# One exponential over two neighbouring weight tiles in the encoder of a graph-attention kernel

## The chip, the cores and the metric

The kernel runs on one core of a Trainium2 chip. The metric is the device time of one execution in microseconds. Everything is float32 but the adjacency mask, which is held in bytes.

## The reference, cut to what matters

Two graph layers run over 4096 nodes with 512 features. The first is an attention autoencoder with four heads, the second a graph-attention layer. The first holds the change:

```python
h = jnp.maximum(_layernorm(x, axis=-1), 0.0)
Xw = jnp.einsum('hnd,hde->hne', Xh, W)                  # 4 heads of 128
f1 = jnp.einsum('hnd,hd->hn', Xw, V[:, 0, :, 0])
f2 = jnp.einsum('hnd,hd->hn', Xw, V[:, 1, :, 0])
sig = jax.nn.sigmoid(f1[:, :, None] + f2[:, None, :])
att = masked_softmax(adj * sig, adj != 0)               # 4096 x 4096 for each head
Xa = jnp.einsum('hij,hjd->hid', att, Xw)                # encoder
emb = mlp_block(batchnorm(Xa), enc_mlp_W, ...)          # elu, residual, batchnorm
Y = jnp.einsum('hij,hjd->hid', att, emb)                # decoder, the same att again
out = mlp_block(elu(Y @ W^T), dec_mlp_W, ...)
```

The exponent of the softmax is a sigmoid, so the kernel makes a weight as exp(0.5 * tanh(0.5 * (f1 + f2))) times the mask; a constant factor falls out in the softmax.

## The kernel before, in words

After a first stage (layer norm, the products with `w0`, the copy of the adjacency into byte masks in DRAM) comes the encoder's attention, then an MLP, the decoder's attention, a second MLP with the next layer's products, and that layer's attention. All three attentions go through the function `attention` (L222).

**A block.** `attention` runs over eight blocks: four heads times two halves of the targets, `TB` = 2048 each. In a block it runs over `NJ` = 32 groups of 128 sources. For each group j it makes a weight tile `e` of 128 sources by 2048 targets and multiplies the 128 values of these sources with it: four matmuls of 512 targets (L377), which add up in four PSUM banks over the 32 groups. The fourth bank comes into use two groups late (L371 to L375).

**A weight tile.** `tanh_weights` (L469) makes it in place with two ScalarE instructions and one of VectorE: a tanh (L471) of the row of target scores `rowb`, with the source's score as a bias for each partition, an exp (L472), and the product with the mask `a` (L473). The mask of a tile, 256 KB, is loaded on SP's queue (L211) into one of five buffers.

**The ring.** `weight_tile` (L253) hands out the tile's place: out of every `EP + ebufs` = 2 + 6 tiles, two come from the pool `keep`, which outlives the encoder, and six from the encoder's own pool. So a ring of eight places of 8 KB a partition goes round, and a tanh has to wait until everything that read the tile eight groups earlier is done.

**Who reads a tile.** The matmuls do, and so does the sum over sources that becomes the softmax's denominator. That sum is made in three ways, by lists of j (`ENC_FIRST`, `ENC_SECOND`, `ENC`): some tiles are added into a second sum by an accumulating DMA on POOL's queue in two halves (L392), some are multiplied with ones on PE (L266), and VectorE adds the others to `acc` (L400, L402). In blocks 2 to 7 eleven tiles go by DMA (j = 0, 2, 5, 7, 10, 12, 15, 17, 20, 22, 25), four by ones (8, 9, 30, 31) and seventeen by VectorE. At the end of a block PE folds both sums into the bank `den`. Every fifth tile is also stored to DRAM (L362), for the decoder: by ACT's queue in blocks 0 and 1, by SP's later.

**The end of a block** is worked off during the next one, at given j: VectorE copies the banks out (L583) and `den` (L272); POOL's queue carries `den` to DRAM (L273), back as columns (L278), VectorE inverts them (L282, L283), POOL's queue stores the inverses (L286) and spreads them over the partitions (L291), and VectorE scales the output (L587) and takes its statistics (L590). POOL's queue goes in order: while it waits for one of these, the accumulating DMAs behind it wait too.

**The order** of each engine's instructions comes from a scheduler that goes by the program's order and its own costs. `pinned` (L214) and `tc.issue_after` put the work of block ends behind given weights.

**The decoder** uses the same function with a ring of 2 + 4 places and reads every fifth tile back instead of making it. Its first two weight tiles lie in `keep`'s places, so that they can be made before the encoder's pool is let go.

Of the kernel before, what the change touches and what calls it, by code (L numbers as in the profile page):

```python
# [31 lines left out]
FP = mybir.dt.float32  # L32
U8 = mybir.dt.uint8
AF = mybir.ActivationFunctionType
ALU = mybir.AluOpType
# [4 lines left out]
N, F, H, D, P = 4096, 512, 4, 128, 128  # L40
IB = 512
NIB = N // IB
NJ = N // P
C = IB // P

TB = 2048
NTB = N // TB
SB = TB // IB
# [8 lines left out]
TINY = 1e-30  # L57
# [15 lines left out]
EP = 2  # L73
# [12 lines left out]
def kernel(ctx, tc, x, xT, adjT, w0, w0T, v0, wencT, wdecT, vecs, w1, w1T, a1, outT):  # L86
    nc = tc.nc
# [46 lines left out]
    score = consts.tile([P, 2, NTB, H, NJ // NTB], FP, name="score")  # L134
# [4 lines left out]
    def column(t, j, h):  # L139
        j = j % (NJ // NTB), j // (NJ // NTB)  # L140
        return t[:, j[1], h, j[0]:j[0] + 1]
# [10 lines left out]
    bias = consts.tile([P, C], FP, name="bias")  # L152
# [68 lines left out]

    def attention(what, keep, pools, weights, values, row_of, out, finish, ebufs, modes=None, invert=None,  # L222
                  kept=None, sums=None, sums2=None, extras={}, row0=None, masks0=(), in_parts0=1,
                  finish_last=None, behind=()):

# [18 lines left out]


        spool, made, masks0 = pools, 0, list(masks0)
        if invert is not None:
            acc = spool.tile([P, TB], FP, name="acc") if sums is None else sums  # L250
            sums2 = (spool.tile([P, TB], FP, name="acc2"), None) if sums2 is None else sums2

        def weight_tile():  # L253
            nonlocal made
            made += 1
            if (made - 1) % (EP + ebufs) < EP:
                return keep.tile([P, TB], FP, name="e", tag="ek", bufs=EP)
            return spool.tile([P, TB], FP, name="e", bufs=ebufs)


        hop = nc.scalar if kept is None else nc.gpsimd
# [60 lines left out]
        later, last_ones, last_main, products_of = {}, None, None, ()  # L322
        rowb = row0 if row0 is not None else next_row_of(0, 0)
        blocks = [(h, tb) for h in range(H) for tb in range(NTB)]
        for n, (h, tb) in enumerate(blocks):
# [8 lines left out]
            for j in range(NJ):  # L334
# [4 lines left out]
                with pinned([a_load, *products_of, last_main] if j else []):  # L339
                    if (n, j) in extras:  # L340
                        extras[n, j](a_load)
                    if not last and j == NJ - 10:
                        next_row = next_row_of(*blocks[n + 1])
                e = weight_tile()
                store = j % KEEP == KEEP - 1 and kept is not None
                if store and kept == "read":
                    a_load = nc.sync.dma_start(e, ekeep[h][tb][j // KEEP])
                else:
                    if masks0:
                        a, a_load = masks0.pop(0)  # L350
                    else:
                        a = mask_tile(keep)
                        a_load = load_mask(a, tb, j)

                    with pinned([*(products_of[:1] if kept == "read" and n == 0 and j < 8 else ()),
                                 *(behind if n == 0 and j < EP else ())]):
                        products_of = weights(e, rowb, a, j, h, SB if NJ * n + j < in_parts0 else 1)


                    if stores and (store if n > 1 else j % KEEP == KEEP - 3):  # L360
                        k, t = stores.pop()
                        (nc.sync if n > 1 else nc.scalar).dma_start(ekeep[h][tb][k], t)  # L362
                    if store:
                        stores.append((j // KEEP, e))
# [60 lines left out]
            if not last:  # L425
# [5 lines left out]
                rowb = next_row  # L431
# [37 lines left out]
    def tanh_weights(e, rowb, a, j, h, parts):  # L469
# [3 lines left out]
            last_dve = nc.vector.tensor_mul(e, e, a)  # L473
        return last_act, last_dve

    a_att, b_att, a_mlp, b_mlp = (coefs[:, k, :] for k in range(4))

    with tc.tile_pool(name="keep", bufs=1) as keep:

        with tc.tile_pool(name="f_small", bufs=1) as small, tc.tile_pool(name="f_work", bufs=2) as work:  # L480
            xs = []
# [4 lines left out]
            for ib in range(NIB):  # L486
# [7 lines left out]
                for c in range(0, C, 1 if ib == 0 else C):  # L494
                    n = 1 if ib == 0 else C
# [11 lines left out]
            for ib in range(NIB):  # L507
# [15 lines left out]
                for c in range(C):  # L523
                    if ib == 0 and c == 1:
# [3 lines left out]
                    made = (nc.gpsimd if by_pool else nc.vector).tensor_scalar(  # L528
                        hn, xs[ib][:, c, :], mv[:, c, 0:1], rstd[:, c:c + 1], ALU.subtract, ALU.mult)
# [23 lines left out]
                for c in range(C):  # L553
                    j = ib * C + c
# [12 lines left out]
                if ib == SB - 1:  # L567
                    store_rows(rows[0], targets(0))
                    row0 = keep.tile([P, TB], FP, name="rowb", bufs=2)
                    row0_load = load_row(row0, rows[0], 0)  # L570
                    with tc.issue_after(row0_load.ins):
                        masks0 = []
                        for j in range(5):
                            a = mask_tile(keep)
# [46 lines left out]
        with tc.tile_pool(name="enc", bufs=1) as spool:  # L621

            with tc.issue_after(last_copy.ins), tc.issue_after(masks0[-1][1].ins):
                attention("enc", keep, spool, tanh_weights, R[0:4], lambda h, tb: (rows[tb], h), out_enc,
                          (scaled, statistics), 6, lambda n: (ENC_FIRST, ENC_SECOND, ENC)[min(n, 2)],
                          (TINY, ALU.max), "write", row0=row0, masks0=masks0,
                          extras={(2, 8): encoder_weights, (H * NTB - 1, 10): coefs_of_three,
                                  (H * NTB - 1, 12): bias_of_three, (H * NTB - 1, 20): scale_three})

# [43 lines left out]
        with tc.tile_pool(name="m_small", bufs=1) as small, tc.tile_pool(name="m_work", bufs=3) as work:  # L673
# [8 lines left out]
            behind_it = []  # L682
# [46 lines left out]
        nc.sync.dma_start(w, wdecT.rearrange("(c p) o -> p c o", p=P))  # L729
        with tc.tile_pool(name="dec", bufs=1) as spool:  # L730
            attention("dec", keep, spool, tanh_weights, xc, lambda h, tb: (rows[tb], h), out_dec, (scaled, elu), 4,
                      kept="read", behind=behind_it, extras={(1, 6): sums_of_weights, (1, 16): bias_of_decoder})


    v1 = xd
# [2 lines left out]
    with tc.tile_pool(name="l_small", bufs=1) as small, tc.tile_pool(name="l_work", bufs=2) as work:  # L738
# [41 lines left out]
        for fb in range(C):  # L780
            with tc.issue_after(last_pe.ins):
                for h in range(H):
                    k = 2 * (fb * H + h)
# [232 lines left out]
```

## Time and profile before

| | |
|---|---|
| time, median of 3 runs (3245.06 to 3245.82) | 3245.78 us |
| span of the profiled execution, first to last instruction | 3243.0 us |
| what the median has beyond that span | 2.8 us |
| PE busy in the span | 3189.8 us (98%) |
| VectorE (DVE) busy | 2665.7 us (82%) |
| ScalarE (ACT) busy | 2582.4 us (80%) |
| encoder's attention | about 58 to 1038 us |
| tanh, L471, 128x2048 | 462 times, 1990 ns each |
| exp, L472, 128x2048 | 462 times, 1901 ns each |
| product with the mask, L473 | 470 times, 2260 ns each |
| TensorE clock granted | 0.997 |

The profile gives no time of its own for the profiled execution other than its span. Its rows tell the engine, the line, the operation, the tiles it writes and reads, their sizes and how often it ran; then the busy time or the mean of one, and the idle time of the engine just before, with what ended it. In a timeline the first number is the start in us from the start of the span, the second the duration. PE's records are halves of a float32 matmul, so four matmuls are eight records. The ends of matmuls are modelled: neighbouring records overlap.

### The profile page before, as it was taken

The numbers are of one execution on the slowest core, as the hardware profiler recorded it, in microseconds if no ns is written. First come the engines' busy times: TensorE is split into PE (matmuls) and PEld (weight loads), VectorE is DVE, ScalarE is ACT, GpSimd is POOL, SyncE is SP. The second block draws the span as 40 slices with busy tenths as digits, with TensorE's granted clock in tenths as the row PEclk, the third lists the DMA queues.
The fourth block names the chain that finished last, engine by engine and source line by source line (L and its number), as shares of the span: only waits on it lengthen the run. The fifth ranks groups of instructions, "written<-read, shape, count | busy, mean of one in ns | idle before, by whom it ended". The sixth has DMA issues, their size and how long they took to land.

```text
span 3243.0 us, 26057 instructions
## 1 busy us (share of the span) xinstructions
PE 3189.8 (98%) x8707; PEld 1480.1 (46%) x8707; DVE 2665.7 (82%) x1946; ACT 2582.4 (80%) x1825; POOL 478.3 (15%) x624
## 2 busy tenths in 40 slices
PE   7999999999999999999999999999999999999998
PEld 6334444444444464444444444448644444444443
DVE  7989999999998765555655665585699999999998
ACT  7999999999997559899999999566765656665663
POOL 3001211211210000000000000025412222122221
PEclk9999999999999999999999999999999999999999
DMA  9998988988985024444443443231489999899996
GB/s 211 198 198 243 276 225 230 270 225 227 265 240 150 7 72 143 136 130 136 142 151 126 128 154 126 73 124 59 127 206 221 208 231 236 217 216 234 232 211 160
DMA packets 212023, 580.60 MB, mean 179 GB/s; under 512 B 25168, under 2 KB 28272, under 8 KB 195888
## 3 DMA queue, kind: packets, MB, share of 16 engines
q0 software_dynamic: 68256, 223.56, 36.4%
q1 hardware_dynamic: 132200, 332.53, 30.2%
q10 hardware_dynamic: 11432, 22.85, 2.0%
q8 instruction: 68, 1.11, 0.1%
q14 instruction: 67, 0.55, 0.0%
HBM read 378.15 MB, written 84.30 MB: 143 GB/s over the span
## 4 chain that ended last, share of the span: by engine, by line
PE 50%; DVE 26%; issue 13%; DMA 6%; ACT 4%; DVEq 0%; POOL 0%; ACTq 0%; POOLq 0%; SPq 0%
PE ps L377 36%; DVE e L933 8%; DVE R L402 8%; PE ps L639 7%; DVE e L473 4%; DVE acc L402 3%; PE ps L838 3%; DMA a<-mask 3%; DMA acc<-e 2%; ACT e L471 2%; ACT e L472 1%; DMA w<-e 1%; PE den L266 1%; PE ps L699 1%; PE ps L374 1%
## 5 line engine op out<-in xcount | busy, mean ns | idle before, releaser
L377 PE MATMUL ps<-e,R 128*128 128x512 f32 x6008 | 2608.3, 595 | 25.8 <-DVE e L473 21.5
L377 PEld LDWEIGHTS ps<-e,R 128*128 128x128 f32 x6008 | 1137.4, 190 | 1490.2 <-issue 1395.7
L473 DVE TENSOR_TENSOR e<-e,a 128x2048 f32<-128x2048 f32 (+1 forms) x470 | 1053.0, 2260 | 392.4 <-ACT e L472 369.4
L471 ACT ACTIVATE e<-rowb,score 128x2048 f32<-128x2048 f32 (+1 forms) x470 | 911.8, 1968 | 82.9 <-PE ps L377 45.4
L472 ACT ACTIVATE e<-e 128x2048 f32<-128x2048 f32 (+1 forms) x470 | 869.3, 1879 | 8.0 <-DVE e L473 2.7
L932 ACT ACTIVATE e<-rowb,nq,jcol 128x2048 f32<-128x2048 f32 x224 | 459.6, 2088 | 262.4 <-DMA w<-e 143.5
L933 DVE SCALAR_TENSOR_TENSOR e<-e,jcol,a 128x2048 f32<-128x2048 f32 (+1 forms) x265 | 592.6, 2269 | 2.8 <-ACT e L932 2.8
L402 DVE TENSOR_TENSOR R<-R,e 128x2048 f32<-128x2048 f32 x128 | 292.3, 2283 | 0.0
L402 DVE TENSOR_TENSOR acc<-acc,e 128x2048 f32<-128x2048 f32 x121 | 276.3, 2283 | 0.9
L392 POOL DMA_DIRECT2D w<-e x178 | 149.4, 845 | 611.4 <-DMA w<-e 285.0
L639 PE MATMUL ps<-R,w 128*128 128x512 f32 x512 | 220.3, 592 | 0.6 <-DVE w L597 0.6
L392 POOL DMA_DIRECT2D acc<-e x146 | 122.7, 891 | 521.8 <-DMA acc<-e 217.3
L291 POOL DMA_DIRECT2D rb<-rinvs x60 | 34.0, 571 | 1055.9 <-DVE R L587 871.5
L639 PEld LDWEIGHTS ps<-R,w 128*128 128x128 f32 x512 | 97.2, 190 | 122.7 <-issue 117.4
L660 ACT ACTIVATE ex<-ps,bias 128x512 f32<-128x512 f32 x64 | 44.0, 688 | 100.7 <-PE ps L639 80.9
L838 PE MATMUL ps<-w1x,hT 128*128 128x260 f32 x512 | 115.5, 384 | 1.4 <-ACT hT L816 1.4
L838 PEld LDWEIGHTS ps<-w1x,hT 128*128 128x128 f32 x512 | 96.5, 190 | 19.9 <-issue 3.3
L932 ACT ACTIVATE e<-w,nq,jcol 128x2048 f32<-128x2048 f32 (+1 forms) x41 | 67.4, 1711 | 24.6 <-DMA R<-e 24.5
L875 POOL TENSOR_TENSOR vacc<-vacc,R 128x128 f32<-128x128 f32 x120 | 65.9, 579 | 45.2 <-ACT R L868 44.9
L662 DVE SCALAR_TENSOR_TENSOR ex<-ex,re 128x512 f32<-128x512 f32 x64 | 44.9, 702 | 32.8 <-ACT re L661 32.7
L868 ACT ACTIVATE R<-ps,rstd 128x128 f32<-128x128 f32 x128 | 38.6, 371 | 29.2 <-PE ps L838 25.5
L266 PE MATMUL den<-e,ones 128*32 128x512 f32 x416 | 51.7, 608 | 3.2 <-DVE e L933 3.2
(176 smaller groups left out, 1239.6 us busy)
## 6 DMA issues: line engine op xcount, KB each, us to landing
a<-mask SPq DMA_DIRECT2D x720, 256.0 KB, 4.1
w<-e POOLq DMA_DIRECT2D x178, 512.0 KB, 6.7
acc<-e POOLq DMA_DIRECT2D x146, 512.0 KB, 7.0
e<-ekeep SPq DMA_DIRECT2D x48, 1024.0 KB, 4.9
ekeep<-e SPq DMA_DIRECT2D x36, 1024.0 KB, 7.0
mask<-in_adjT POOLq DMA_DIRECT2D x8, 2048.0 KB, 104.7
rowb<-rows SPq DMA_DIRECT2D x16, 1024.0 KB, 5.4
rb<-rinvs POOLq DMA_DIRECT2D x60, 256.0 KB, 4.7
```

The lines of the kernel that those rows point to most:

```text
L266: last_ones = nc.tensor.matmul(den[s * 32:(s + 1) * 32, :], ones[:, 0:32], t[:, s * IB:(s + 1) * IB], start=start, stop=stop)
L377: last_main = nc.tensor.matmul(b, block(values[h], j), e[:, s * IB:(s + 1) * IB], start=(j == 0), stop=(j == NJ - 1))
L392: nc.gpsimd.dma_start(into_half, e_half, **({"accum_op": ALU.add} if j > moved[0] else {}))
L402: nc.vector.tensor_add(acc, acc, e)
L471: nc.scalar.activation(e, rowb, AF.Tanh, bias=column(score[:, 1], j, h), scale=0.5)
L472: last_act = nc.scalar.activation(e, e, AF.Exp, scale=0.5)
L473: last_dve = nc.vector.tensor_mul(e, e, a)
L639: last = nc.tensor.matmul(z, w[:, fb, o * P:(o + 1) * P], nodes(src[fb], ib), start=(fb == 0), stop=(fb == C - 1))
L838: m = nc.tensor.matmul(banks[k][:, 0:2 * DX], hT[:, fb, c * P:(c + 1) * P], w1x[:, fb, 2 * k:2 * k + 2, :].rearrange("p h x -> p (h x)"), ...
L875: nc.gpsimd.tensor_add(vacc[:, h, :], vacc[:, h, :], block(v1[h], j))
L932: last_act = nc.scalar.activation(e, rowb, AF.Relu, bias=column(nq, j, h), scale=column(jcol, j, h))
L933: last_dve = nc.vector.scalar_tensor_tensor(e, e, column(jcol2, j, h), a, ALU.add, ALU.mult)
```

## The change

Both parts of the ring become one tensor each: `ring`, two places, in `keep`, for the encoder and the decoder; and `ring2`, six places, in the encoder's pool. A place is a slice of its tensor.

In the encoder, all tiles but the first two are made in pairs (j even and j + 1). At the even j, `slots_of_two` takes two neighbouring places, and `tanh_pairs` writes two tanhs into them, each with its own bias, and then one exp over both, 4096 elements a partition. The product with the mask stays one instruction for each tile, at its own j. The places of a pair are separate slices, so each is waited for and let go by itself. The decoder keeps `tanh_weights`; it takes its two kept places from `ring`, too. The third attention is as before.

```diff
+        ring2 = spool.tile([P, ebufs, TB], FP, name="er") if pairs is not None else None
...
         def weight_tile():
             nonlocal made
             made += 1
-            if (made - 1) % (EP + ebufs) < EP:
-                return keep.tile([P, TB], FP, name="e", tag="ek", bufs=EP)
-            return spool.tile([P, TB], FP, name="e", bufs=ebufs)
+            k = (made - 1) % (EP + ebufs)
+            if k < EP:
+                return ring[:, k, :] if ring is not None else keep.tile([P, TB], FP, name="e", tag="ek", bufs=EP)
+            return ring2[:, k - EP, :] if pairs is not None else spool.tile([P, TB], FP, name="e", bufs=ebufs)
+
+        def slots_of_two():
+
+            nonlocal made
+            k = made % (EP + ebufs)
+            made += 2
+            return ring[:, k:k + 2, :] if k < EP else ring2[:, k - EP:k - EP + 2, :]
...
-                e = weight_tile()
+                by_two = pairs is not None and n * NJ + j >= EP
+                if not by_two:
+                    e = weight_tile()
+                elif j % 2:
+                    e = two[:, 1, :]
+                else:
+                    two = slots_of_two()
+                    e = two[:, 0, :]
...
-                        products_of = weights(e, rowb, a, j, h, SB if NJ * n + j < in_parts0 else 1)
+                        if not by_two:
+                            products_of = weights(e, rowb, a, j, h, SB if NJ * n + j < in_parts0 else 1)
+                        else:
+                            if j % 2 == 0:
+                                last_act = pairs(two, rowb, j, h)
+                            products_of = last_act, nc.vector.tensor_mul(e, e, a)
...
+    def tanh_pairs(two, rowb, j, h):
+
+        for k in range(2):
+            nc.scalar.activation(two[:, k, :], rowb, AF.Tanh, bias=column(score[:, 1], j + k, h), scale=0.5)
+        both = two.rearrange("p k i -> p (k i)")
+        return nc.scalar.activation(both, both, AF.Exp, scale=0.5)
...
     with tc.tile_pool(name="keep", bufs=1) as keep:
+        ring = keep.tile([P, EP, TB], FP, name="ek")
...
-                          (TINY, ALU.max), "write", row0=row0, masks0=masks0,
+                          (TINY, ALU.max), "write", row0=row0, masks0=masks0, ring=ring, pairs=tanh_pairs,
...
-                      kept="read", behind=behind_it, extras={(1, 6): sums_of_weights, (1, 16): bias_of_decoder})
+                      kept="read", behind=behind_it, ring=ring, extras={(1, 6): sums_of_weights, (1, 16): bias_of_decoder})
```

More of the change, by code (lines that the diff above doesn't have):

```diff
@@ L223, in attention @@
                   kept=None, sums=None, sums2=None, extras={}, row0=None, masks0=(), in_parts0=1,
-                  finish_last=None, behind=()):
+                  finish_last=None, behind=(), ring=None, pairs=None):
         spool, made, masks0 = pools, 0, list(masks0)
+        ring2 = spool.tile([P, ebufs, TB], FP, name="er") if pairs is not None else None
         if invert is not None:
```

## The prediction

> **What bounds the kernel now.** I read the engine table, then the busy time by stage, because the change touches only the encoder's attention (58 to about 1038 us of the span). Blocks are the eight (head, half) passes of that loop, n = 0 to 7. The view of stages gives one block a row (columns: PE, PEld, DVE, ACT, POOL, then clock and DMA). First the page's engine line, then two of these stages:
>
> ```profile
> PE 3189.8 (98%) x8707; PEld 1480.1 (46%) x8707; DVE 2665.7 (82%) x1946; ACT 2582.4 (80%) x1825; POOL 478.3 (15%) x624
> ```
>
> ```profile
> 555.00:673.00 118.00, 116.56 (x304) 49.50 (x304) 114.16 (x63) 118.00 (x65) 22.39 (x29) 1.00 0.89 241
> 673.00:791.00 118.00, 116.56 (x304) 49.50 (x304) 114.15 (x64) 118.00 (x65) 22.36 (x29) 1.00 0.89 241
> ```
>
> The page as a whole says PE. These stages say ACT: 118.00 of 118.00 us, with PE 1.4 us and DVE 3.9 us short of full. The view of waits for ACT alone has no entry at all from 405 to 1026 us. Before that, from 192 us, it has:
>
> ```profile
> ACT e L471 <- PE den L266: 4.5, 4, 2.0
> ACT e L471 <- DMA acc<-e: 2.7, 2, 2.5
> ACT e L472 <- DVE e L473: 2.7, 3, 1.3
> ```
>
> So until 400.35 us (the last of these waits) ACT is held by the ring: it waits for a place that PE's ones-products or an accumulating DMA has not yet let go. From then on it runs without a pause. Its rhythm, in the timeline of ACT (start, duration), first in the encoder, then in the decoder:
>
> ```profile
> 597.90 3.88 ACT L471 ACTIVATE e<-rowb,score 128x2048 f32<-128x2048 f32 x2
> 601.69 3.70 ACT L472 ACTIVATE e<-e 128x2048 f32<-128x2048 f32 x2
> 605.29 3.88 ACT L471 ACTIVATE e<-rowb,score 128x2048 f32<-128x2048 f32 x2
> ```
>
> ```profile
> 1499.21 1.99 ACT L471 ACTIVATE e<-rowb,score 128x2048 f32<-128x2048 f32 x1
> 1501.23 1.91 ACT L472 ACTIVATE e<-e 128x2048 f32<-128x2048 f32 x1
> 1503.04 1.99 ACT L471 ACTIVATE e<-rowb,score 128x2048 f32<-128x2048 f32 x1
> ```
>
> Two tanhs, two exps, 605.29 - 597.90 = 7.39 us for a pair of tiles, 16 pairs 118.2 us: the block. In the decoder an exp stands right behind the tanh that it reads, and starts 2.02 us after it instead of 1.89: such a direct dependence costs 0.13 us.
>
> PE at its fastest: 64 records of L377 take 27.47 us in the chain that ended last, 0.429 each; a block has 256, so 109.9, and 48 ones records at 3.57/32, so 5.4: 115.2 us. PE is next, 3.0 us below ACT.
>
> **What the Trainium skill says.** "ScalarE: Activation LUTs", What ACT_TABLE_LOAD costs: an ACTIVATE with immediate operands takes 186 ns + 0.833 ns per element, a pointer bias adds about 93, and neighbours overlap by about 93. The trace agrees: 1.99 us for tanh (pointer bias), 1.90 for exp, and starts 1.89 and 1.80 apart. Its Table sets section puts tanh and exp in one set; no load stands between them here. "Perfetto Trace Analysis", Identifying the Most-Contended Engine, warns that matmul busy time is no measure of PE's headroom: hence the 115.2 from spacing above. "DMA: Bandwidth & Descriptors", Rules for kernel authors: an accumulating DMA must wait for the earlier one's semaphore. The trace has 217 us of POOL waiting for `acc<-e` landings in the encoder: a serial chain.
>
> **The change part by part.**
>
> *Fewer exps.* 127 pairs lose two exps of 2048 and gain one of 4096. No 4096 form is in the trace; by the page it is 186 + 3412 - 93 = 3505 ns from start to start (an estimate), against 2 x 1800. Gain 0.093 us a pair (bounds: 0, if the second half brings its own start-up; 0.186, if nothing overlapped). I take 0.093.
>
> *Order on ACT.* In the built program 114 of the 127 double exps stand behind one tanh of the next pair, 13 right behind their own second tanh. Those 13 pay 0.13 each (bounds 0 and 0.25), and the tanhs queued behind them with them; DVE alone waits for the exp itself. A steady block has 16 pairs and two such: 16 x 0.093 - 2 x 0.13 = 1.23, so 118.2 becomes 117.0, still above PE's 115.2 and DVE's 114.2.
>
> *What of it counts.* Up to 400.35 us ACT is held by the ring, and a gain there only lengthens the wait. From there (tile 89 of 256) I count to where the end is decided. From 909.54 us, the last tile of block 6, PE runs without a gap to the end of the encoder:
>
> ```profile
> 905.14 3.70 PE L377 MATMUL ps<-e,R 128*128 128x512 f32 x8 [0.70 <-DVE e L473]
> 907.21 6.68 DVE L473 TENSOR_TENSOR e<-e,a 128x2048 f32<-128x2048 f32 x3
> ...
> 909.54 2.84 PE L377 MATMUL ps<-e,R 128*128 128x512 f32 x6 [0.70 <-DVE e L473]
> ```
>
> That start is set by DVE, which last waited for ACT (0.69 us, in DVE's timeline) at 847 us, tile 16 of block 6. Pairs from tile 89 to there: 60 x 0.093 = 5.6, less 8 direct ones x 0.13 = 1.0: 4.5 us, unrounded. What ACT gains later PE doesn't pass on.
>
> *Later first product.* A pair's multiplications now wait for both tanhs, one more tanh, and the double exp: 3 x 1.89 + 3.60 = 9.3 us after the first tanh, against 5.7 (two tanhs, one exp). DVE runs 3.6 us further behind ACT, for both tiles, since the second product follows the first. At the start of the encoder this is covered: DVE there waits 12.0 us in all for masks. Wherever DVE follows ACT again (after 346 us) it is paid once, not per block, and is still there at 907 us: +3.6. Bounds 1.8 (if the extra tanh weren't ahead) and 4.0. Cover gone at the start, nothing more: the same shift isn't paid twice.
>
> *Places freed one by one.* The waits in the built program stand at each tanh for its own place (accumulate semaphores only where that place's last user was accumulated), so the wider tiles add none. But a double exp is queued behind the first tanh of the next pair, and its wait for a place. Nobody waits there after 405 us now. The nearest place is one read by an accumulating DMA, on POOL's queue, block 5:
>
> ```profile
> 705.41 0.58 POOL L286 DMA_DIRECT2D rinvs<-dcol  x1 [1.80 <-DVE dcol L283]
> 710.49 1.63 POOL L291 DMA_DIRECT2D rb<-rinvs  x3 [4.49 <-DMA rinvs<-dcol]
> 712.10 1.85 POOL L392 DMA_DIRECT2D acc<-e  x2
> 721.35 0.84 POOL L392 DMA_DIRECT2D acc<-e  x1 [7.40 <-DVE acc L402]
> ```
>
> POOL waits for DVE's reciprocal, and everything behind it, down to tile 15's accumulate (second half issued at 734.20, landed 743.6), moves by DVE's 3.6. Tile 23's tanh, which takes that place, starts at 747.53: slack 3.9 us. It also comes 0.9 us sooner in its block (24 tanhs x 0.04), so 4.5 of slack is asked for. By the same reckoning blocks 4 and 6 have 5.7 and 4.9, block 7 over 8. One block misses by 0.6; with landings that scatter (2.9 to 11.4 us there) I take 1.0 us (bounds 0 and 12). In block 2, where the chain binds already, rinvs isn't waiting for DVE, so nothing moves.
>
> *PE, SP and the decoder.* PE's order is unchanged; DVE's too in blocks 3 to 6; SP moves one row load by one place; POOL moves one accumulate a block past a neighbour. The decoder keeps its single exps; only the name of its two kept tiles changes. All costed at nothing.
>
> **Sum.** Against the profiled execution: -4.5 + 3.6 + 1.0 = +0.1 us on a span of 3243.0. The median of the runs, 3245.78, is 2.8 above that span (what lies outside first and last instruction), which I carry over: 3245.9.
>
> **Rivals.** *No change that can be told (forecast, 0.74).* As above. What a measurement of this kernel can tell is about 0.2%, 6.5 us.
>
> *Faster (0.06).* The latency isn't paid, because PE's last stretch starts elsewhere, and the ring's waits before 400 us shrink too: all 127 pairs, 11.8 - 13 x 0.13 = 10.1 us, 3235.7. For it: ACT is full. Against: PE has 3 us a block left and is without a gap in block 7.
>
> *Slower (0.20).* The accumulate chain takes ACT's place as the bound. Place: the tanhs of tiles 20, 23 and 25 of blocks 3 to 6, behind POOL's wait for DVE. It decides from where the slack falls below 4.5 us. If landings there are 2 to 3 us later than now, each of four blocks loses some 3 us: 3245.9 - 1.0 + 12 = 3256.9. For it: slack 3.9 in block 5, and DMA engines 89% busy. Against: the shift is paid as a delay once a block, and most landings have more room.
>
> *That it doesn't do what it says:* excluded, the 127 double exps are in the program.
>
> **How the numbers follow.** Faster by over 0.2% 0.06, within 0.74, slower 0.20. Range 3242.0 (the shift at its low bound 1.8 and no stall, with some of the early gain) to 3254.0 (9 us of stall): about 0.05 is left out below and 0.13 above.
>
> **What would show it.** Double exps of 3.60 us, 7.30 us a pair; blocks of 117.0 us; no ACT wait or one of about a microsecond on `acc<-e` after 405 us; PE waiting longer for DVE, and the MLP starting within a microsecond of before. Wrong: 2 us or more of ACT waits a block on `acc<-e` (slower), or the last PE stretch starting 4 us earlier (faster).

## The result and the profile after

The changed kernel takes 3255.03 us (median of 8 runs, 3250.91 to 3259.51) against 3245.59 for the kernel before (median of 8, 3242.94 to 3248.11): ratio 1.0031, 95% interval 1.0022 to 1.0040. That is 9.4 us slower, where +0.1 was forecast, and 1.0 us above the range that was given. Run again later, beside 34 runs of the kernel before, it gave 1.0028 (1.0017 to 1.0038). The profiled execution took 3250.91 us, the shortest of the eight; its span is 3249.1, 6.1 more than before, so the trace shows less than the whole 9.4.

The page of the changed kernel first: the engines, then the tanhs of pairs (L500) and the double exps (L502), with busy time, mean in ns and idle time ahead of them. These rows have the tiles in the six places of `ring2`, named `er`; the 62 tanhs and 31 double exps in the two places of `ring`, named `ek`, are counted apart.

```profile
PE 3186.5 (98%) x8707; PEld 1478.8 (46%) x8707; DVE 2665.2 (82%) x1946; ACT 2572.1 (79%) x1698; POOL 478.2 (15%) x624
...
L500 ACT ACTIVATE er<-rowb,score 128x2048 f32<-128x2048 f32 x192 | 376.6, 1991 | 20.6 <-DMA acc<-er 16.4
...
L502 ACT ACTIVATE er<-er 128x4096 f32<-128x4096 f32 x96 | 346.3, 3607 | 0.4
```

ACT does 10.3 us less, as it should, and the time is longer all the same. The idle column of L500 says where to look: the tanhs waited 20.6 us, 16.4 of them for an accumulating DMA to have read the place that they were to write. The steady rhythm, in ACT's timeline of the changed kernel:

```profile
594.40 3.60 ACT L502 ACTIVATE er<-er 128x4096 f32<-128x4096 f32 x1
597.91 3.88 ACT L500 ACTIVATE er<-rowb,score 128x2048 f32<-128x2048 f32 x2
601.70 3.60 ACT L502 ACTIVATE er<-er 128x4096 f32<-128x4096 f32 x1
```

A pair takes 601.70 - 594.40 = 7.30 us, the double exp 3.51 from start to start (3505 ns was the estimate from "ScalarE: Activation LUTs", What ACT_TABLE_LOAD costs). So the local gain is there. The view of stages, for the same two stretches as before (they are no longer whole blocks), and the waits of ACT from 192 to 1026 us:

```profile
555.00:673.00 118.00, 116.87 (x307) 49.88 (x306) 114.93 (x64) 117.94 (x50) 22.45 (x29) 1.00 0.88 241
673.00:791.00 118.00, 116.90 (x307) 50.03 (x306) 115.25 (x65) 117.88 (x49) 22.47 (x29) 1.00 0.89 241
```

```profile
ACT er L500 <- DMA acc<-er: 16.4, 7, 7.1
ACT ek L500 <- DVE acc L421: 3.0, 1, 3.0
```

ACT is as full as before there, with PE and DVE doing a little more in 118 us: the work goes faster. The waits that it now has, 16.4 us on accumulates against 2.7, are longest where the prediction had not looked. When each block's last product on DVE ended tells where the rest went (us from the start of the span, one profiled execution each):

| block | 0 | 1 | 2 | 3 | 4 | 5 | 6 | 7 |
|---|---|---|---|---|---|---|---|---|
| before | 191.6 | 314.6 | 434.7 | 554.9 | 673.1 | 791.3 | 909.5 | 1025.3 |
| changed | 194.9 | 322.9 | 447.5 | 564.9 | 682.2 | 799.2 | 918.5 | 1031.8 |
| changed, later | +3.3 | +8.3 | +12.8 | +9.9 | +9.1 | +7.9 | +9.0 | +6.5 |

All of the loss is made in blocks 0 to 2, the stretch that the prediction had set aside as held by the ring anyway. Blocks 3 to 5 win some back, 1.2 us in block 5, where nothing stalls. PE's last matmul of the loop ends at 1038.2 us instead of 1030.2; the two MLPs and the third attention last as long as before to within 0.5 us, and the decoder, whose instructions are the same, came out 1.7 shorter in this execution.

Block 0's 3.3 us are the lateness of the pairs: the first product of a pair starts at 77.90 us instead of 74.28. The waits of DVE for masks, from 58 to 320 us, did not take it up. The first line is before, the other two are changed:

```profile
DVE e L473 <- DMA a<-mask: 12.0, 10, 2.9
DVE er L378 <- DMA a<-mask: 8.2, 5, 3.2
DVE ek L378 <- DMA a<-mask: 3.5, 3, 1.5
```

In block 1 the products of tiles 18 and 19 end 2.6 us later than before, and those of tiles 20 to 23 8.0 to 8.1 us. That jump of 5.4 us is one event. ACT of the changed kernel, then DVE, then POOL (the accumulate at 254.54 is tile 14's, two halves of 512 KB):

```profile
261.27 1.99 ACT L500 ACTIVATE er<-rowb,score 128x2048 f32<-128x2048 f32 x1
270.40 2.00 ACT L500 ACTIVATE er<-rowb,score 128x2048 f32<-128x2048 f32 x1 [7.14 <-DMA acc<-er]
...
272.31 3.60 ACT L502 ACTIVATE er<-er 128x4096 f32<-128x4096 f32 x1
```

```profile
268.29 2.28 DVE L423 TENSOR_TENSOR acc<-acc,er 128x2048 f32<-128x2048 f32 x1
275.94 2.29 DVE L378 TENSOR_TENSOR er<-er,a 128x2048 f32<-128x2048 f32 x1 [5.37 <-ACT er L502]
```

```profile
250.99 0.55 POOL L295 DMA_DIRECT2D rinvs<-dcol  x1 [3.64 <-DVE dcol L292]
252.95 1.62 POOL L300 DMA_DIRECT2D rb<-rinvs  x3 [1.41 <-DMA rinvs<-dcol]
254.54 1.90 POOL L413 DMA_DIRECT2D acc<-er  x2
```

Tile 22's tanh (270.40) waited 7.1 us for the place that tile 14 had, because the accumulate that reads tile 14 landed only then. The double exp at 272.31 is that of tiles 20 and 21. Both of its tanhs were done at 263.3; it stood behind tile 22's tanh in ACT's queue, and DVE had nothing to do until it was done. In the kernel before, the two exps of tiles 20 and 21 stood ahead of tile 22's tanh (ACT), and tile 20's product began at 267.90 (DVE), 8.0 us earlier:

```profile
261.36 3.70 ACT L472 ACTIVATE e<-e 128x2048 f32<-128x2048 f32 x2
264.96 2.00 ACT L471 ACTIVATE e<-rowb,score 128x2048 f32<-128x2048 f32 x1
```

```profile
267.90 2.28 DVE L473 TENSOR_TENSOR e<-e,a 128x2048 f32<-128x2048 f32 x1
```

And POOL had tile 14's accumulate ahead of the inverses:

```profile
248.25 1.83 POOL L392 DMA_DIRECT2D acc<-e  x2 [3.46 <-DVE e L473]
250.60 0.58 POOL L286 DMA_DIRECT2D rinvs<-dcol  x1 [0.53 <-DVE dcol L283]
259.38 1.63 POOL L291 DMA_DIRECT2D rb<-rinvs  x3 [8.20 <-DMA rinvs<-dcol]
```

The accumulate was issued at 248.25 there and landed some 10.6 us later, about 6 us before tile 22's tanh began. Two orders have changed at once: the accumulate has moved behind three loads of 256 KB, and an exp that used to stand ahead of the waiting tanh stands behind it. The experiments take them apart.

### The profile page after: what moved, and what is told of

It is laid out like the page before. It is cut to its first block, busy times and chain, and to the rows that moved or that the text cites. A ratio compares the mean times of both kernels' runs of the same rounds, so it can differ in the third digit from the quotient of the medians.

```text
span 3249.1 us, 25850 instructions
## 1 busy us (share of the span) xinstructions
PE 3186.5 (98%) x8707; PEld 1478.8 (46%) x8707; DVE 2665.2 (82%) x1946; ACT 2572.1 (79%) x1698; POOL 478.2 (15%) x624
## 4 chain that ended last, share of the span: by engine, by line
PE 52%; DVE 24%; issue 12%; DMA 8%; ACT 4%; DVEq 0%; POOL 0%; ACTq 0%; SPq 0%; POOLq 0%
PE ps L398 38%; PE ps L668 7%; DVE e L962 5%; DVE R L423 5%; DMA a<-mask 5%; DVE er L378 4%; DVE acc L423 4%; PE ps L867 3%; DVE ek L378 2%; DMA acc<-er 2%; ACT er L502 1%; PE ps L728 1%; DMA w<-e 1%; ACT er L500 1%; PE den L275 1%
## 5 line engine op out<-in xcount | busy, mean ns | idle before, releaser
L398 PE MATMUL ps<-e,R 128*128 128x512 f32 x3324 | 1441.1, 593 | 2.0 <-DVE e L962 1.8
L398 PEld LDWEIGHTS ps<-e,R 128*128 128x128 f32 x3324 | 629.8, 190 | 803.9 <-issue 777.1
L398 PE MATMUL ps<-er,R 128*128 128x512 f32 x1528 | 671.8, 597 | 21.2 <-DVE er L378 15.6
L398 PE MATMUL ps<-ek,R 128*128 128x512 f32 x1156 | 511.1, 594 | 12.3 <-DVE ek L378 8.4
L494 DVE TENSOR_TENSOR e<-e,a 128x2048 f32<-128x2048 f32 x138 | 315.5, 2292 | 234.8 <-ACT e L493 227.1
L398 PEld LDWEIGHTS ps<-er,R 128*128 128x128 f32 x1528 | 288.4, 191 | 400.1 <-issue 353.5
L378 DVE TENSOR_TENSOR er<-er,a 128x2048 f32<-128x2048 f32 x192 | 433.0, 2284 | 36.6 <-ACT er L502 28.4
L500 ACT ACTIVATE er<-rowb,score 128x2048 f32<-128x2048 f32 x192 | 376.6, 1991 | 20.6 <-DMA acc<-er 16.4
L502 ACT ACTIVATE er<-er 128x4096 f32<-128x4096 f32 x96 | 346.3, 3607 | 0.4
L492 ACT ACTIVATE e<-rowb,score 128x2048 f32<-128x2048 f32 x138 | 274.1, 1992 | 57.4 <-PE ps L398 29.9
```

The source lines that it names most:

```text
L378: products_of = last_act, nc.vector.tensor_mul(e, e, a)
L398: last_main = nc.tensor.matmul(b, block(values[h], j), e[:, s * IB:(s + 1) * IB], start=(j == 0), stop=(j == NJ - 1))
L492: nc.scalar.activation(e, rowb, AF.Tanh, bias=column(score[:, 1], j, h), scale=0.5)
L500: nc.scalar.activation(two[:, k, :], rowb, AF.Tanh, bias=column(score[:, 1], j + k, h), scale=0.5)
L502: return nc.scalar.activation(both, both, AF.Exp, scale=0.5)
```

## The experiments

The kernel before was timed again beside each group of runs: 3244.77, 3245.32, 3245.03, 3244.69 and, for the last two kernels, 3245.00 and 3246.16. Each ratio below is against the runs beside it.

**Is it the fixed order of places?** The ring tensors fix each tile's place to that of the tile eight back; before, a tile came from one of two pools, and no trace tells which place in it the tile had. The first run keeps the tensors and makes no pairs:

```diff
-                by_two = pairs is not None and n * NJ + j >= EP
+                by_two = False
```

> The encoder takes its tiles from the two ring tensors of the changed kernel, in their fixed order (each tile the place of the tile 8 back), but every tile keeps its own exp of 2048. The order of instructions on each engine is that of the kernel before. Theory A (the loss comes from the pairs: products 3.6 us later from the first block on, and in blocks 1 and 2 a pair must hold two free places before its exp): no loss to speak of, within 2 us of the kernel before (3245.6): at 264.96 us, where tile 22 of block 1 starts its tanh, the accumulate of tile 14 has landed some 6 us earlier. Theory B (the loss comes from the fixed order of places, which takes away the scheduler's choice of a place that is free sooner): some 8 to 9 us slower, about 3254.5, with ACT waiting for an accumulate in blocks 1 and 2 as in the changed kernel.

Measured 3244.33 us, ratio 0.9998 (0.9990 to 1.0006). The order of places costs nothing that could be told; theory B falls.

**Which blocks?** The same line with `n >= 3` (pairs in blocks 3 to 7 only), and with `n < 3` added to the condition of the change.

> Pairs with the double exp only in blocks 3 to 7; blocks 0 to 2 keep single exps, on the ring tensors with their fixed order of places. Theory A: the end of block 2's products stays where it is in the kernel before (434.7 us, within 1.5), then 3.6 us of lateness is paid once at the first pair, blocks 3 to 6 win 1.2 us each, and 2 to 3 us are lost in block 6 to an accumulate: 3244 to 3247, no difference that can be told. Theory B: the end of block 2 comes 8 us or more later, and the whole takes 3253 to 3255.

> Pairs with the double exp only in blocks 0 to 2 (from tile 2); blocks 3 to 7 have single exps on the ring tensors. Theory A: the end of block 2's products comes about 12 us later than in the kernel before, as in the changed kernel; 3.6 of it (the lateness of the products against ACT) comes back when single exps begin in block 3, nothing else does: 3252 to 3256. Theory B: the same loss, by the order of places: this run alone does not part A from B, it says whether the whole loss is made before block 3, and together with the run of pairs from block 3 it adds up to the changed kernel.

Measured: pairs from block 3 on 3246.74, ratio 1.0005 (0.9997 to 1.0014); pairs up to block 2 3252.23, ratio 1.0023 (1.0015 to 1.0031). 2.0 and 7.5 us add up to the 9.4 of the whole. In the first of the two, products come 2.7 us later at the first pair of block 3 and 1.2 earlier again in block 4, which is what the prediction's sum described. In the second, 6.0 us of 13.5 come back in block 3, where single exps begin. So nothing speaks against the sum for blocks 3 to 7, and most of the loss is made before.

**Lateness without the wider exp.** Two exps of 2048 after the two tanhs, and the first product waits for the second exp (the lines that make it wait are left out here):

```diff
-        both = two.rearrange("p k i -> p (k i)")
-        return nc.scalar.activation(both, both, AF.Exp, scale=0.5)
+        for k in range(2):
+            last = nc.scalar.activation(two[:, k, :], two[:, k, :], AF.Exp, scale=0.5)
+        return last
...
```

> As the changed kernel, but the double exp is two exps of 2048 (tanh, tanh, exp, exp), and the first product of a pair still waits for the second exp: the pair's lateness stays, the shorter ACT work is taken away. Theory A: at least as slow as the changed kernel, since only the gain of about 1.2 us a block falls away: ACT 118.2 us or a little more in blocks 3 to 7, first products 1.8 to 2 us later (no tanh of the next pair stands ahead of the exp), the stalls of blocks 1 and 2 somewhat smaller than there (3 to 8 us in all), and nothing won back later: 3249 to 3256. Theory B: 8 to 9 us lost in blocks 1 and 2, the same as with single exps, and nothing won back: about 3256. Theory C (the width of the exp itself costs, by what else uses the memory during 3.6 us): back to about 3246.

Measured 3246.55, ratio 1.0006 (0.9998 to 1.0014), below what theory A expected. Its first pair is 1.8 us late, not 3.6, because here no tanh of the next pair stands ahead of the exp, and block 1 has no jump at tile 20 although the accumulate of tile 14 lands as late (ACT waited 2.3 us for it, until 269.8). So neither a lateness of this size nor the late landing is enough, and the order on ACT became the suspect.

**The order on ACT, everywhere and up to block 2.** No tanh of a pair is issued before the double exp of the pair ahead; the second kernel does this with `and n < 3`:

```diff
-                                last_act = pairs(two, rowb, j, h)
+                                with pinned([last_double] if last_double is not None else []):
+                                    last_double = last_act = pairs(two, rowb, j, h)
```

> As the changed kernel, but no tanh of a pair may be issued before the double exp of the pair ahead (order tanh, tanh, double exp, everywhere). Theory A1 (what hurts in blocks 1 and 2 is that a double exp stands in ACT's queue behind the first tanh of the next pair, which waits for its place: tile 22 of block 1 holds up the products of 20 and 21, tile 10 of block 2 those of 8 and 9): products 1.8 us late instead of 3.6, no jump at tile 20 of block 1 (5.4 us in the changed kernel) nor at tile 8 of block 2 (3.5 us), end of block 2's products 2.5 to 5 us later than in the kernel before (434.7 us) instead of 12.8. Each double exp now follows its own tanh directly and costs 0.13 more: blocks of 118.6 to 118.7 us, so 2 to 3 us lost in blocks 3 to 7: 3248 to 3251 in all. Theory A2 (the late landing of the accumulate itself is the loss, whatever stands behind the waiting tanh): the jumps stay, 3254 to 3257.

> As the changed kernel, but in blocks 0 to 2 no tanh of a pair is issued before the double exp of the pair ahead; from block 3 on the order of the changed kernel. Theory A1: blocks 0 to 2 as in the run with that order everywhere (end of block 2's products 2.5 to 5 us later than in the kernel before), then 1.8 us more of lateness, less what the ring gave away in block 2, less 1.2 us in each of blocks 3 to 6: 3245.5 to 3248. Theory A2: the jumps of blocks 1 and 2 stay: 3253 to 3255.

Measured 3253.29, ratio 1.0026 (1.0016 to 1.0037), and 3249.26, ratio 1.0013 (1.0006 to 1.0020). The jump at tile 20 falls to 0.8 us in both, as A1 has it. The first gives that back: with every double exp right behind its own second tanh, a block takes about 0.8 us more than before, where 0.4 to 0.5 was expected. Both miss their times, by 2.3 and 1.3 us. POOL's order also moved in them (tile 14's accumulate went ahead of two of the three loads), so they don't part the two causes.

**POOL's order alone.** In block 1 the store of the inverses, and so its loads, are put behind the accumulate of tile 14; every other instruction of every engine stays in its place (`last_moved` is the latest accumulate; the lines that keep it, and one that moves the store's turn in the program, are left out):

```diff
-            hop.dma_start(rinvs[h][tb].rearrange("o (p k) -> (o p) k", k=TB // P), dcols[0])
+            with pinned([last_moved] if last_moved is not None and n == 1 else []):
+                hop.dma_start(rinvs[h][tb].rearrange("o (p k) -> (o p) k", k=TB // P), dcols[0])
...
```

> As the changed kernel, but in block 1 the accumulate of tile 14 stands on POOL ahead of the store and the three loads of the inverses, where it stood in the kernel before; every other instruction keeps its place. Theory A3 (the place it was moved to is the cause in block 1: it is issued behind three loads of 256 KB and lands 15.7 us after its issue, against 10.6 before): it lands near 264 us instead of 270.2, tile 22's tanh waits under 1.5 us instead of 7.1, the jump at tile 20 (5.4 us) is nearly gone, block 2 still loses its 5 us: about 3249.5 to 3251.5. If only the lateness of the products counts (theory A without the order): as the changed kernel within 1.5 us, 3253.5 to 3256.5.

Measured 3249.76, ratio 1.0011 (1.0004 to 1.0017): by the medians 5 us of the 9.4 are back. POOL and, in the second fence, ACT of this run:

```profile
254.04 1.82 POOL L414 DMA_DIRECT2D acc<-er  x2 [5.79 <-DVE er L379]
255.16 1.28 POOL L296 DMA_DIRECT2D rinvs<-dcol  x1
```

```profile
265.11 2.01 ACT L501 ACTIVATE er<-rowb,score 128x2048 f32<-128x2048 f32 x1 [0.26 <-DMA acc<-er]
```

The accumulate is issued 0.5 us earlier than in the changed kernel and lands 5.3 us earlier; tile 22's tanh waits 0.26 us instead of 7.14, and there is no jump.

**Is the move dear by itself?** It is brought alone into the version with single exps (`by_two = False`, as in the first run): the accumulate of tile 14 behind the store and two of the loads. The helper that issues it is left out here.

```diff
-                    if j in moved:
+                    if kept == "write" and (n, j) == (1, 14):
+                        at(16, accumulate_behind, into, e)
+                    elif j in moved:
...
```

> Single exps everywhere on the fixed places (as in the first run, 3244.3), with one move: in block 1 the accumulate of tile 14 stands on POOL behind the store and two of the loads of the inverses. If the move costs by itself: it lands at 266 to 270 us instead of 259, tile 22's tanh (264.96 us) waits 1 to 5 us, and 1 to 5 us are lost, 3245.5 to 3249. If it costs only because the pairs come late and ask for the place early: within 1 us of the first run.

Measured 3244.99, ratio 1.0001 (0.9993 to 1.0009): no loss that could be told, although the landing is as late as in the changed kernel. ACT and DVE of this run, tile 22's tanh being the one at 270.42:

```profile
262.05 3.69 ACT L501 ACTIVATE er<-er 128x2048 f32<-128x2048 f32 x2
270.42 2.00 ACT L500 ACTIVATE er<-rowb,score 128x2048 f32<-128x2048 f32 x1 [4.68 <-DMA acc<-er]
```

```profile
266.38 2.29 DVE L431 TENSOR_TENSOR acc<-acc,er 128x2048 f32<-128x2048 f32 x1
268.58 2.29 DVE L502 TENSOR_TENSOR er<-er,a 128x2048 f32<-128x2048 f32 x1
```

The same tanh waits until the same time, to within 0.02 us. But the exps of tiles 20 and 21 (262.05) are out before the wait, and DVE goes from one instruction to the next without a gap.

**The queue on ACT alone.** Two neighbours on ACT are to be exchanged in the changed kernel, POOL left as it is. The first try pinned tile 22's tanh behind the double exp ahead of it, and the scheduler put another tanh, tile 24's, ahead of that exp. So this kernel is not what its expectation describes.

> As the changed kernel, with two neighbours on ACT exchanged: in block 1 the double exp of tiles 20 and 21 stands ahead of tile 22's tanh instead of behind it. Nothing else moves; the accumulate of tile 14 stays behind the loads of the inverses. If the queue on ACT is what costs: tile 22's tanh still waits, to about 270 us, but DVE no longer waits 5.4 us for the double exp, products of 20 and 21 come about 2.7 us later than in the kernel before instead of 8, and 3 to 5 us come back: 3250 to 3252. If the late landing costs by itself: only the products of 20 and 21 come earlier, those of 22 and after stay 8 us late: 3253.5 to 3256.

Measured 3251.10, ratio 1.0021 (1.0011 to 1.0031). Tile 24's tanh waited 4.1 us for PE ahead of the exp, and the jump at tile 20 was 2.5 us, against 7.1 and 5.4: 3.0 less wait, 2.9 less jump. The second try pins both tanhs. Its trace has every instruction of the encoder in the changed kernel's order, but for that one exp:

```diff
-                                last_act = pairs(two, rowb, j, h)
+                                with pinned([last_act] if (n, j) in ((1, 22), (1, 24)) else []):
+                                    last_act = pairs(two, rowb, j, h)
```

> As the changed kernel, with two neighbours on ACT exchanged and nothing else: in block 1 the double exp of tiles 20 and 21 stands ahead of tile 22's tanh (order: tanh 21, double exp 20 and 21, tanh 22, tanh 23, double exp 22 and 23, tanh 24). If the queue on ACT is what costs: tile 22's tanh still waits for the late accumulate, to about 270 us, DVE does not wait 5.4 us for the double exp of 20 and 21 (under 1 us), the products of 20 and 21 come 2 to 3.5 us later than in the kernel before instead of 8, and 3 to 5 us come back: 3250 to 3252. If the late landing costs by itself: the products of 22 and after stay 7 to 8 us late: 3253.5 to 3256.

Measured 3248.56, ratio 1.0007 (0.9999 to 1.0016). By the medians one exchange of two instructions brings back some 7 us of 9.4 (9.4 - 2.4, each against the runs beside it), and no difference from the kernel before is left that could be told. ACT, then DVE:

```profile
263.56 1.99 ACT L501 ACTIVATE er<-rowb,score 128x2048 f32<-128x2048 f32 x1
265.58 3.63 ACT L503 ACTIVATE er<-er 128x4096 f32<-128x4096 f32 x1
270.71 2.00 ACT L501 ACTIVATE er<-rowb,score 128x2048 f32<-128x2048 f32 x1 [1.50 <-DMA acc<-er]
```

```profile
268.88 2.29 DVE L424 TENSOR_TENSOR acc<-acc,er 128x2048 f32<-128x2048 f32 x1
271.08 2.29 DVE L379 TENSOR_TENSOR er<-er,a 128x2048 f32<-128x2048 f32 x1
```

The accumulate still lands at about 270.7. Only what stands behind the waiting tanh is different, and DVE has no gap: the product of tile 20 comes 3.2 us later than before, about what a pair costs anyhow.

The traces show the jump gone, not the gain at the end. The profiled executions of this kernel (3252.16) and of the one with POOL's order (3253.16) are each the second longest of theirs. Both have block 1's products end 3.4 and 4.3 us later than before instead of 8.3; but then ACT waits 6.3 and 5.8 us for accumulates at tile 20 of later blocks, and block 7's end 5.0 and 5.8 us later, not far from the changed kernel's 6.5. That the gain reaches the end rests on the medians.

**Block 2.** There the changed kernel loses another 4.5 us of product time, in waits of the same kind (tile 10's tanh, 2.9 us, with the double exp of 8 and 9 behind it). The order on ACT was mended in block 2 alone, and together with POOL's order in block 1 (the pinning line above with `n == 2`):

> As the changed kernel, but in block 2 only no tanh of a pair is issued before the double exp of the pair ahead. A1: block 1 as in the changed kernel (jump of 5.4 us at tile 20), the jump of 3.5 us at tile 8 of block 2 is gone and 2 to 3 us come back: 3251.5 to 3253. A2: 3254 to 3256.

> As the changed kernel, with the accumulate of tile 14 of block 1 ahead of the inverses (as in the run of that alone, 3249.8) and, in block 2 only, no tanh of a pair issued before the double exp of the pair ahead. If the double exps queued behind waiting tanhs are a part of block 2's loss (theory A1): products of block 2 end 2 to 3 us nearer to the kernel before than in the run with POOL's order alone (there 5.2 us are added between the first and the last product of block 2), 3246.5 to 3248.5. If not (A2, the chain of accumulates alone): 3249 to 3250.5.

Measured 3255.54, ratio 1.0032 (1.0021 to 1.0043), and 3251.33, ratio 1.0019 (1.0012 to 1.0027): nothing won in either. In the trace of the first the jump at tile 8 is gone and block 2 loses 2.7 us instead of 4.5; but at the end of block 3 both kernels stand at +9.9 and +10.0. What block 2's products lost that way comes back in block 3 anyhow. A1 is right on what happens there and wrong on its being worth time. In the second, block 1's jump is gone as well, and 6.6 us are lost all the same.

**Other tiles for the accumulates.** Odd tiles only, as many as before (in the changed kernel, in the kernel before, and, from block 3 on only, in the version with pairs from block 3 on):

```diff
-ENC_SECOND = (12, 14, 17, 19, 22, 24, 26), (1, 2, 4, 5, 7, 8, 30, 31)
-ENC = (0, 2, 5, 7, 10, 12, 15, 17, 20, 22, 25), (8, 9, 30, 31)
+ENC_SECOND = (13, 15, 17, 19, 23, 25, 27), (1, 2, 4, 5, 7, 8, 30, 31)
+ENC = (1, 3, 5, 7, 11, 13, 15, 17, 21, 23, 25), (8, 9, 30, 31)
```

> As the changed kernel, but the accumulating DMAs read odd tiles only (block 1: 13, 15, 17, 19, 23, 25, 27; later blocks: 1, 3, 5, 7, 11, 13, 15, 17, 21, 23, 25), as many as before. The place of an odd tile is asked for by the second tanh of a pair, which stands behind the double exp ahead, not in front of it, and some 5.4 us later. Theory A1: nothing is held up any more at tile 20 of block 1 nor at tile 8 of block 2, the waits of ACT on accumulates fall from 16 us to under 5 us in all, only the lateness of 3.6 us is paid and 1.2 us a block comes back: 3244 to 3247.5. Theory A2 (the chain of accumulates as a whole can't keep up with products that come 3.6 us later, whichever tiles it reads): 3252 to 3256.

> Control: the kernel before with the same odd tiles for its accumulating DMAs. Theory A1: its exps and tanhs alternate so that no pair is held up, and its waits on accumulates are 2.7 us in all, so within 2 us of the kernel before, 3243 to 3246.5. If it gains 5 us or more too, the list of tiles is better on its own account and the run with pairs says nothing on the pairs.

> Pairs from block 3 on, as in the earlier run of that kind (3246.7), with odd tiles for the accumulating DMAs from block 3 on. Theory A1: the accumulate waits of blocks 3 to 6, which took back the 1.2 us a block there in most runs, go away; what is left is 2.8 us of lateness paid at block 3 and 4 times 1.2 us gained: 3242 to 3244, a version under both kernels. If the accumulates of blocks 3 to 6 weren't the cause: 3245.5 to 3248 as before.

Measured 3254.20, ratio 1.0030 (1.0020 to 1.0041); 3246.26, ratio 1.0005 (0.9997 to 1.0013); 3250.33, ratio 1.0019 (1.0011 to 1.0026). The jump at tile 20 is gone in the first, and the waits have moved to tiles 23 and 25, in blocks 1, 2, 4 and 6. The list is no better than the old one in the changed kernel, worse with pairs from block 3 on (3250.3 against 3246.7), and makes no difference with single exps. The expectation of the first and third failed: the exp is out of the way, but tiles 23 and 25 now wait for places that accumulates still read; why the loss is as large as before is not shown. The control adds to the case for the queue: with single exps tile 22's tanh waited 5.3 us for an accumulate, and the product of tile 20 was not later.

**The scatter, and a version below both.** The changed kernel once more, and pairs in blocks 3 and 4 only (`n in (3, 4)`):

> The changed kernel once more, unaltered, beside the three runs that follow, to see which of its waits come back: 3253.5 to 3256.5. If the stalls of blocks 1 and 2 are the stable part, its trace has again a wait of 6 us or more at tile 22 of block 1 and 2 to 4 us at tile 10 of block 2; if the stalls of blocks 3 to 6 are what scatters from run to run, they are elsewhere and of another size than the 0.3, 2.4 and 0.9 us of the first profile.

> Pairs with the double exp in blocks 3 and 4 only, single exps before and after. Theory A (the lateness of 3.6 us is paid when pairs begin and comes back when they end; each block of pairs gives ACT 1.2 us): products of block 4 end about 1.2 us later than in the kernel before, as in the run of pairs from block 3; block 5's come back to 2 to 2.4 us earlier, and PE has blocks 5 and 6 to catch up: encoder 1.5 to 2.5 us shorter, 3242.5 to 3243.5, against 3244.8. Rival (PE can't catch up at 3.6 us a tile, or the ring takes the gain): 3244.5 or more.

The first gave 3254.36, with 6.75 us of wait at tile 22 of block 1 and 3.0 at tile 10 of block 2, where the first profile had 7.14 and 2.89; after 405 us it has one wait on an accumulate, of 0.2 us, where the first profile had three, of 3.6 in all. So blocks 1 and 2 are the lasting part and the later waits scatter. The second gave 3244.84, ratio 1.0000 (0.9992 to 1.0008): products 2.1 us later at the end of block 4, 2.2 earlier in block 5 (the lateness comes back), but no time won that could be told. No version beat both kernels.

## Why the prediction was wrong, point by point

- *Fewer exps, order on ACT.* Right: 3.51 us against 3505 ns, a pair 7.30, a steady block 117.0 (682.2 to 799.2). A double exp right behind its own tanh starts 265.58 - 263.56 = 2.02 us after it, so the 0.13 holds for the wide form too.
- *Later first product, 3.6 us.* Right in size: 3.6 at the first pair, tile 2 of block 0. Wrong on the place: "At the start of the encoder this is covered: DVE there waits 12.0 us in all for masks". DVE waits for masks there as long as before (11.7 us): a mask's buffer comes free by the product that reads it (SP's mask loads wait 207 and 206 us for products there in the two kernels), so the masks come later too, and the lateness stays. "Paid once" is right: it comes back where pairs end.
- *What of it counts: "Up to 400.35 us ACT is held by the ring, and a gain there only lengthens the wait."* This is the step that failed. It prices a gain in that stretch at nothing, and no term of the sum prices a delay there. Pairs in blocks 0 to 2 alone cost 7.5 of the 9.4 us. In block 1 tile 14's accumulate had landed some 6 us before tile 22's tanh began; with tile 14's product later and the loads ahead, it landed 11 to 12 us later, and ACT waited 7.1.
- *POOL moves one accumulate a block past a neighbour: costed at nothing.* Wrong with the pairs: in block 1 that neighbour is a store and three loads, and putting the accumulate back is worth 5 us by the medians. With single exps a late landing made by such a move is indeed free.
- *Places freed one by one.* The mechanism was named ("a double exp is queued behind the first tanh of the next pair, and its wait for a place") and then priced after 405 us only. "PSUM — Partial Sum Buffer", Engine vs sequencer instructions, calls ScalarE's queue strictly first in, first out; the exp at 272.31 us shows it. Its price is the wait, less what DVE has left to do: 7.14 us of wait gave 5.4 of lost product time, 4.1 gave 2.5, and about 0 when the exp stood ahead.
- *In block 2 "nothing moves".* Wrong as it stands, products lose 4.5 us there; but some of it is given back in block 3, and two runs that changed the order there won no time.
- *The 1.0 us in blocks 3 to 6.* Within its bounds: 3.6 us of waits after 405 us in one execution of the changed kernel, 0.2 in the other. The whole sum, +0.1, can't be told from the run with pairs from block 3 on (+2.0, with an interval from -1 to +4.5), nor from the changed kernel once the two instructions are exchanged (+2.4); there it is in part luck, since that kernel's products are still 8.4 us late at the end of block 2.
- *The rival on the slow side* had the cause, an accumulate's landing, and the wrong place: tiles 20, 23 and 25 of blocks 3 to 6, with four times 3 us. The lasting part was one tile of block 1, so that its 3256.9 lies near the measured 3255.03 is luck. Waits in its place do occur, most at tile 20: between 0.2 and 6.3 us in all after 405 us in the profiled executions of the changed kernel, of the exchange and of POOL's order. No run prices them.

Open: what remains of the 9.4 us without block 1's jump isn't divided further between the lateness, block 2 and the scattered waits. Leaving out the odd tiles and ACT's order everywhere, which lose time in other places, the kernels without that jump and with the double exps still lose 2.4 (the exchange), 3.9 (ACT's order up to block 2), 4.4 (POOL's order) and 6.6 us (POOL's order and ACT's in block 2), so the jump is worth 3 to 7 us, not a sharp figure. The runs with pairs spread over 4 to 12 us (3242.25 to 3254.46 for the kernel with POOL's order), the kernel before over 4 to 7. A larger ring, which might take the wait away, wasn't tried.

## What to carry to other kernels

A stretch that waits on a ring is not a stretch that can be ignored: a delay cost time there where a gain would not have won any, and whoever shifts a producer has to recompute each wait there first. When instructions are merged, look at what the scheduler now puts between the merged instruction and its inputs: an instruction that waits for a buffer, standing ahead of finished work on the same engine, holds up that work; here exchanging the two gave most of the loss back, by the medians. A change of order on a DMA queue that costs nothing in one version can cost in another: with single exps the late landing made a tanh wait 4.7 us and nothing was lost, because the exps that DVE needed were already done.

## What the hardware showed that wasn't expected

- The same accumulate (two halves of 512 KB) landed 15.9 us after its issue behind three loads of 256 KB (254.54 to 270.40), and 11.1 us after it with nothing of POOL's just ahead (254.04 to 265.11), each taken to the start of the tanh that waited for it alone.
- The store of the inverses, 8 KB, landed 1.4 to 2.5 us after POOL came to the wait for it where it stands ahead of that accumulate (the changed kernel, and the one with single exps and the accumulate moved), and 8.2 to 9.0 us where it stands behind (the kernel before, and the changed one with POOL's order). So in either order one of the two is late. "DMA: Bandwidth & Descriptors", Rules for kernel authors, says that DMAs of different issuing engines share the same 16 DMA engines and interleave; both of these are POOL's, and how they share the engines is not shown here.
